# Decays kept as one row per head, the first tiles reordered, and an early pool for y and w_o in the last head unit of a lightning-attention kernel

## The chip, the cores and the metric

The kernel runs on one core of one Trainium2 chip. The core has a matmul engine (PE, with its weight loads shown apart as PEld), a vector engine (DVE), a scalar engine (ACT), GpSimd (POOL) and SP, which here only issues DMAs. The metric is the device time in microseconds of one execution; lower is better. All data are float32 in and out.

## The reference

The input is four sequences of 512 tokens with 512 features. It is normalised, goes through a linear attention with 16 heads of 128 and a decay per head, and the result is multiplied by a gate that comes from a router and added to the input.

```python
def reference(x, slope, w_qkv, w_gate, w_out, norm_w, router_w, router_b, expert_b):
    xn = layernorm(x)                                  # 4 x 512 x 512
    q, k, v = split(silu(xn @ w_qkv.T))                # 16 heads of 128
    # per head, in causal order, with s the head's slope:
    #   o[m] = sum over n <= m of exp(-s*(m-n)) * (q[m].k[n]) * v[n]
    o = norm_w * rms_normalise(o)                      # over all 2048 features
    a = (sigmoid(xn @ w_gate.T) * o) @ w_out.T
    p = softmax(xn @ router_w.T + router_b)            # 64 experts
    w, i = top_k(p, 8)
    g = silu(xn * sum(w) + sum_k w[k] * expert_b[i[k]])
    return x + a * g
```

The reference works in blocks of 64 tokens; the kernel uses blocks of 128 (`P`), which gives the same sums.

## The kernel before, in words

The program is one hand-written order of instructions for five engines. Each engine runs its own queue in program order; semaphores tie them together. The file's order is therefore the schedule: a list `after[0..6]` says what is emitted behind each of a unit's products.

**Products.** A float32 product is made of three passes over operands split into a high and a low part (`PASSES`; `split_hi` is a copy on ACT, `split_lo` a subtraction on DVE or POOL). A unit (`unit`, line 478) multiplies a 2x2 block of weights with a 2x2 block of tokens in seven products instead of eight (`PRODUCTS`: A11·B11, S2·T2, S1·T1, A12·B21, S3·T3, S4·B22, A22·T4), with six matmuls each. The S are sums of weight blocks, the T sums of token blocks. The first two units (`plain_unit`, line 519) take eight products instead, since their sums aren't there yet; in these T1 stands for the block B12. `do_deferred` emits the product with the sigmoid that an earlier sink has left open.

**V stage (lines 879 to 981).** Sixteen units, k = 0 to 15, make v. Eight token tiles (pairs of two sequences, 128 tokens each) go by in order with the first half of w_v (`ws[0]`), and then all again with the second half (`ws[1]`). Each tile is prepared while the one before is multiplied (`prepare`, line 816): `stats` and rstd (DVE, then POOL), `norms` (DVE), `turn` (transposes on PE, two copies on ACT, a store of the transposed tile), `sums`, `plain` and `more` (sums and splits of the token blocks), and `logits` (16 router matmuls). Four buffers hold x, four hold the finished v (`vout`).

**Decays.** `make_dist` builds a 128x256 table of token distances on POOL. `make_decays` takes its exponential for each head, 128x256, on ACT. `mask_decays` sets the upper triangle of the first half to zero on POOL and stores each head's table in DRAM by SP. In the head stage `load_decay` fetches one head's table.

**Head stage (lines 984 to 1062).** 48 units: for each of two pairs of sequences, a gate unit for two heads and then a q-k unit for each. `attention` of a head is emitted within the next unit: `scores_qk` behind product 1, `states` behind product 3, `attend` behind product 6. `attend` makes y = o * norm * gate (DVE), stores y in DRAM (SP), squares o (ACT) and adds the square up (POOL). Of the seven split token blocks of the second pair, four lie in the pool `xc` and three in `xa`. The PSUM pool `ps_sc` has three banks.

**Output stage (lines 1064 to 1123).** 32 steps, (sequence, head): y is loaded, split and multiplied with w_o (`o_head`, 12 matmuls a step). `ahead(i, loads, splits)` keeps loads and splits some steps ahead. The last head's attention sits in the first three steps (`last_steps`). In step 3 the head stage's pools are closed and the pool `late` is opened, which takes the loads from then on. `load_eb` and `split_eb` fetch and split the router's bias, `ffn` uses it.

Of the kernel before, what the change touches and what calls it, by code (L numbers as in the profile page):

```python
# [8 lines left out]
F32 = mybir.dt.float32  # L9
# [5 lines left out]
P = 128  # L15
# [35 lines left out]
def kernel(  # L51
# [61 lines left out]
    dist = const.tile([P, 2, P], F32, tag="dist", name="dist")  # L113
    rest_of = const.tile([P, 1], F32, tag="rest_of", name="rest_of")
# [5 lines left out]
    decay_d = [dram.tile([P, 2, P], F32, tag=f"decay{h}", name=f"decay_{h}") for h in range(NH)]  # L120
# [28 lines left out]

    def make_dist():  # L150
        nc.gpsimd.iota(
            dist[:, 0, :], pattern=[[-1, P]], base=0, channel_multiplier=1,
            allow_small_or_imprecise_dtypes=True,
        )
        nc.gpsimd.iota(
            dist[:, 1, :], pattern=[[-1, P]], base=-1, channel_multiplier=0,
            allow_small_or_imprecise_dtypes=True,
        )
        nc.gpsimd.iota(
            rest_of, pattern=[[0, 1]], base=1 - P, channel_multiplier=1,  # L160
            allow_small_or_imprecise_dtypes=True,
        )
        nc.gpsimd.tensor_scalar(dist[:, 0, :], dist[:, 0, :], 0.0, None, ALU.min)


    def make_decays(d, hs):
        for h in hs:
            nc.scalar.activation(d[h // 4][:, h % 4], dist, AF.Exp, scale=slopes[:, h : h + 1])

    def mask_decays(d, hs):  # L170
        for h in hs:
            nc.gpsimd.affine_select(
                d[h // 4][:, h % 4, 0], d[h // 4][:, h % 4, 0], pattern=[[1, P]],
                compare_op=ALU.is_ge, fill=0.0, base=0, channel_multiplier=-1,
            )
        for h in hs:
            nc.sync.dma_start(out=decay_d[h], in_=d[h // 4][:, h % 4])
# [69 lines left out]
    def transpose(stage, p, j, t):  # L247
# [6 lines left out]
        nc.scalar.copy(xfs[p, t][:, j], pt)  # L254
# [53 lines left out]
    def logits(stage, p, t):  # L308
        if t == 0:
            scores[p] = stage.tile([P, PB, NT, E], F32, tag="scores", name=f"scores_{p}", bufs=2)  # L310
        ps = ps_sc.tile([P, PB, E], F32, tag="sc", name=f"lg_{p}_{t}")
        for j in range(PB):
            for c in range(FC):
                nc.tensor.matmul(  # L314
                    ps[:, j], xfs[p, t][:, j, c, :], rw[:, c, :], start=(c == 0), stop=(c == FC - 1)
                )
        nc.vector.tensor_tensor(
# [331 lines left out]
    def load_decay(p, h, attp):  # L649
        dec[p, h] = attp.tile([P, 2, P], F32, tag="dec", name=f"dec_{p}_{h}", bufs=3)  # L650
        nc.sync.dma_start(out=dec[p, h], in_=decay_d[h])
# [86 lines left out]
    def load_eb(outp):  # L738
        ebs.append(outp.tile([P, F], F32, tag="x", name="raw_eb"))
# [29 lines left out]

    wos = {}  # L770
# [17 lines left out]
    def split_wo(h, wop, w):  # L788
        wr = wop.tile([P, 2, F], F32R, tag=f"wr{h}", name=f"wr_{h}", bufs=1)
# [96 lines left out]
    nc.scalar.activation(kdecay[:, 0:NT], mhalf, AF.Exp)  # L886
    nc.scalar.dma_start(out=slopes, in_=slope.to_broadcast([P, NH]))
# [3 lines left out]
    make_dist()  # L891
    warm_up(WARM)
# [3 lines left out]
    for n in ["A21"] + [n for n, _, _, _ in PRODUCTS]:  # L896
        ws[0].place(n)
    nc.scalar.activation(kdecay, slopes, AF.Exp, scale=rest_of[:, 0:1])
    nc.scalar.activation(bdecay, slopes, AF.Exp, scale=-float(P))
    ds = [  # L900
        sump.tile([P, KC * VW], F32, tag=f"sum{i}", name=f"mkdecay_{i}").rearrange(
            "p (h a m) -> p h a m", a=2, m=P
        ) for i in range(4)
    ]
    hs = range(0, 7), range(7, 12), range(12, NH)
    make_decays(ds, hs[0])
    prep[0]["stats"]()
    prep[0]["norms"]()
    ws[0].split_one("A11", nc.vector, hi=True)
    prep[0]["turn"]()  # L910
    load_pair(stage, *tiles[2])
    mask_decays(ds, hs[0])
    warm_up(6)
    prep[0]["sums"]()
    ws[0].split_one("A12", nc.gpsimd, 0)
    ws[0].split_one("A12", nc.vector, 1)
    prep[0]["logits"]()
    prep[1]["stats"]()
    ws[0].split_one("A21", nc.vector)
    make_decays(ds, hs[1])  # L920
    prep[1]["norms"]()
    load_pair(stage, *tiles[3])
    mask_decays(ds, hs[1])
# [245 lines left out]
```

## Time and profile before

| what | value |
|---|---|
| median of 3 runs | 1070.56 us (1069.88 to 1070.57) |
| the profiled execution's own time | 1069.32 us |
| its span, first to last instruction | 1067.6 us |
| instructions | 16505 |
| mean granted TensorE clock | 0.999 |
| DMA | 143.09 MB, 134 GB/s over the span |

The span is what the profiler saw between the first and the last instruction; the execution's own time is 1.7 us longer. The profile page gives busy time by engine, the DMA queues, and the costliest groups of instructions. Other views of the same trace show the busy time of each engine in chosen stretches, who waited for whom, the chain of work that ended last, and the instructions in order of time. A timeline line has the start, the duration, the engine, the line of the kernel, the operation, the tile written and the tiles read, and, in brackets, the idle time of the engine before it and what ended that. Times in these views are microseconds from the span's start. Consecutive instructions of one kind are merged ("x6"). The lines named most are L103 (`split_lo`), L100 (`split_hi`), L496 (matmul of a unit), L552 (product of `silu_of`) and L805 (`o_head`).

### The profile page before, as it was taken

The page shows a single profiled execution, that of the slowest core. Times are in us where ns is not written, and L with a number is a line of the kernel's source. Part 1 is how long each engine was busy: PE and PEld are TensorE (multiplying, and loading weights), DVE is VectorE, ACT ScalarE, POOL GpSimd, SP SyncE. Part 2 cuts the span into 40 slices and gives each one's busy share as a digit, 9 for nine tenths or more (in the row PEclk, how much of TensorE's full clock was granted, in tenths as well). Part 3 has the DMA queues.
Part 4 walks back from the last instruction along what each step waited for, and adds up shares of the span by engine and source line. Part 5 has one row for each costly group of instructions (what it writes and reads, how often), then busy time and mean ns, then how long its engine had stood idle before and what let it go on. Part 6 is the DMA issues. An engine that isn't in the chain of part 4 may idle for free.

```text
span 1067.6 us, 16505 instructions
## 1 busy us (share of the span) xinstructions
PE 1055.7 (99%) x5771; PEld 910.0 (85%) x5771; DVE 691.3 (65%) x1061; ACT 482.3 (45%) x938; POOL 731.0 (68%) x725
## 2 busy tenths in 40 slices
PE   9999999999999999999999999999999999999998
PEld 8788788888888888888888888888888887888886
DVE  5898776667576676655756656557566565754464
ACT  7545545544444444444444444444444444332221
POOL 6898793867788678777786787777867746612130
PEclk9999999999999999999999999999999999999999
DMA  8556745422422223234722242232222428364351
GB/s 273 194 181 241 268 153 178 140 92 85 139 84 94 83 94 111 95 124 171 278 85 66 84 128 85 85 125 88 85 75 88 135 80 285 94 189 173 88 197 50
DMA packets 105203, 143.09 MB, mean 134 GB/s; under 512 B 9120, under 2 KB 53536, under 8 KB 104224
## 3 DMA queue, kind: packets, MB, share of 16 engines
q1 hardware_dynamic: 104112, 141.33, 40.1%
q8 instruction: 46, 0.75, 0.3%
q10 hardware_dynamic: 1008, 0.70, 0.2%
q14 instruction: 37, 0.30, 0.1%
HBM read 91.14 MB, written 50.86 MB: 133 GB/s over the span
## 4 chain that ended last, share of the span: by engine, by line
PE 92%; DVE 3%; DMA 2%; ACT 1%; issue 1%; SPq 1%; POOL 0%; DVEq 0%; ACTq 0%; POOLq 0%
PE u_qk L496 28%; PE po L805 15%; PE u_g L496 14%; PE u_v L496 11%; PE o L702 5%; PE sa L665 5%; PE o L704 4%; PE ss L688 4%; PE kt L668 2%; DMA raw_v<-in_w_v_dram 1%; PE lg L314 1%; DVE vo_v L552 1%; PE pu L759 1%; DMA raw_eb<-in_expert_b_dram 1%; DVE sum_v L432 1%
## 5 line engine op out<-in xcount | busy, mean ns | idle before, releaser
L805 PE MATMUL po<-wr,yr 128*128 128x512 f32 (+1 forms) x777 | 179.7, 388 | 2.2 <-DVE u L798 1.0
L805 PEld LDWEIGHTS po<-wr,yr 128*128 128x128 f32 x777 | 144.2, 188 | 33.0 <-DVE u L798 1.2
L496 PE MATMUL u_qk<-blk_T,ws_qk 128*128 128x512 f32 x576 | 147.1, 395 | 0.0
L714 POOL TENSOR_TENSOR sqs<-sqs,sq 128x512 f32<-128x512 f32 x60 | 78.8, 1314 | 77.2 <-ACT sq L713 77.2
L496 PEld LDWEIGHTS u_qk<-blk_T,ws_qk 128*128 128x128 f32 x576 | 105.7, 188 | 20.4
L103 POOL TENSOR_TENSOR ws_qk<-sum_qk,ws_qk 128x512 fp32r<-128x512 f32 x64 | 82.9, 1297 | 30.4 <-ACT ws_qk L100 29.4
L103 DVE TENSOR_TENSOR yr<-yin,yr 128x512 fp32r<-128x512 f32 x64 | 69.1, 1095 | 47.0 <-ACT yr L100 47.0
L496 PE MATMUL u_qk<-blk_B,wa_qk 128*128 128x512 f32 x384 | 99.2, 393 | 0.0
L552 DVE TENSOR_TENSOR k<-k,sg_k 128x512 f32<-128x512 f32 x64 | 90.8, 1418 | 2.4 <-ACT sg_k L549 2.2
L702 PE MATMUL o<-at,vin 128*128 128x128 f32 x512 | 88.4, 275 | 0.0
L496 PEld LDWEIGHTS u_qk<-blk_B,wa_qk 128*128 128x128 f32 x384 | 70.9, 188 | 14.2
L692 DVE SCALAR_TENSOR_TENSOR st<-st,bdecay,ss 128x128 f32<-128x128 f32 x128 | 41.7, 346 | 60.7 <-ACT st L690 58.4
L549 ACT ACTIVATE sg_k<-k 128x512 f32<-128x512 f32 x64 | 40.5, 632 | 86.4 <-DVE k L487 86.4
L702 PEld LDWEIGHTS o<-at,vin 128*128 128x128 f32 x512 | 74.9, 191 | 2.5
L496 PE MATMUL u_g<-blk_T,ws_g 128*128 128x512 f32 x288 | 76.0, 400 | 0.0
L103 POOL TENSOR_TENSOR ws_g<-sum_g,ws_g 128x512 fp32r<-128x512 f32 x32 | 42.7, 1334 | 46.4 <-ACT ws_g L100 46.4
L704 PE MATMUL o<-qd,st 128*128 128x128 f32 x384 | 74.2, 275 | 0.0
L713 ACT ACTIVATE sq<-o 128x512 f32<-128x512 f32 x60 | 35.9, 598 | 72.3 <-POOL sqs L714 43.5
L767 POOL TENSOR_TENSOR u<-u,sgu 128x512 f32<-128x512 f32 x16 | 20.7, 1292 | 69.7 <-ACT sgu L766 60.4
L706 DVE SCALAR_TENSOR_TENSOR y<-o,nw,gt 128x512 f32<-128x512 f32 x64 | 47.6, 747 | 31.7 <-PE o L704 30.1
L665 PE MATMUL sa<-q,k 128*128 128x128 f32 x512 | 67.7, 275 | 0.2 <-DVE k L552 0.2
L665 PEld LDWEIGHTS sa<-q,k 128*128 128x128 f32 x512 | 64.3, 191 | 3.5 <-DVE q L552 0.7
(182 smaller groups left out, 2429.0 us busy)
## 6 DMA issues: line engine op xcount, KB each, us to landing
v<-vo_v SPq DMA_DIRECT2D x64, 256.0 KB, 2.0
raw_qk<-in_w_head_dram SPq DMA_DIRECT2D x64, 256.0 KB, 4.0
vin<-v SPq DMA_DIRECT2D x64, 256.0 KB, 3.6
y<-y SPq DMA_DIRECT2D x64, 256.0 KB, 2.1
yin<-y SPq DMA_DIRECT2D x64, 256.0 KB, 3.1
x<-in_x_dram SPq DMA_DIRECT2D x32, 256.0 KB, 4.6
raw_g<-in_w_head_dram SPq DMA_DIRECT2D x32, 256.0 KB, 3.1
raw_v<-in_w_v_dram SPq DMA_DIRECT2D x16, 256.0 KB, 5.3
```

The lines of the kernel that those rows point to most:

```text
L103: eng.tensor_tensor(lo, src, hi.bitcast(F32), ALU.subtract)
L496: nc.tensor.matmul(ps, lhsT, rhs, start=(first and c == 0 and n == 0), stop=(c == KC - 1 and n == len(PASSES) - 1), skip_group_check=not f ...
L549: nc.scalar.activation(sg, src, AF.Sigmoid)
L552: nc.vector.tensor_tensor(dst, src, sg, ALU.mult)
L665: nc.tensor.matmul(pa[:, c], k[:, c], q[:, c], start=True, stop=True)
L688: nc.tensor.matmul(ps[:, c], kd[s][:, c], v_of(b, h, c), start=True, stop=True)
L692: nc.vector.scalar_tensor_tensor(r[:, c], r[:, c - 1], bdecay[:, h : h + 1], ps[:, c], ALU.mult, ALU.add)
L702: nc.tensor.matmul(o, v_of(b, h, c), at[s][:, c], start=True, stop=(c == 0))
L704: nc.tensor.matmul(o, st[s][:, c - 1], qd[s][:, c - 1], start=False, stop=True)
L706: nc.vector.scalar_tensor_tensor(y, po, nw[:, h : h + 1], gts[s], ALU.mult, ALU.mult)
L714: nc.gpsimd.tensor_tensor(sq[b], sq[b], s1, ALU.add)
L805: nc.tensor.matmul(pos[t][:, c], yr[:, yi, bass.ts(t, P)], wos[h][:, wi, c], start=(h == 0 and n == 0), stop=(h in stops and n == len(PASS ...
```

## The change

**Decays as one row per head.** The table of a head depends only on the difference of two token positions. The change keeps one row of 256 values per head, 16x256, with zeros in its first 127 places: one exponential for all heads, one memset for the mask. `slope_of`, a column of 16 slopes, is loaded for it. `keep_rows` stores the rows in DRAM in unit 2; `keep_decay` copies a head's row 128 times, DRAM to DRAM, six heads a unit in units 13 to 15. `load_decay` reads two pieces: the first with a step of 255 elements from row to row, so that each row is shifted by one against the row above, the second straight.

**First tiles reordered.** A sigmoid on a small tile follows the exponentials. For tile 0 the transposes of both sequences come first; DVE copies the first out of PSUM, ACT splits B11 straight from PSUM, and POOL makes its low part. The router matmuls of the second sequence move into unit 0. The order of A12's halves on DVE and POOL is exchanged. Tile 1's normalisation comes before the split of A21. Tile 2's statistics are emitted ahead of tile 1's `turn`, and the normalisation of tiles 2 and 3 ahead of the other work of its slot. The splits of S4 of the second half come one product later.

**A pool for y and w_o in the last head unit.** `xc` gets a stack of its own, which is closed behind product 3 of the last head unit; a pool `op2` of four buffers is opened there. Loads and splits of the steps 2 and later use it instead of `late`. Six steps are loaded and three split by the end of the unit. The router's bias is loaded in the unit (into a w_o buffer) and split in step 3. w_o of the heads 4 to 6 goes into the blocks of `xa`, of the later ones into `late`.

```diff
-    dist = const.tile([P, 2, P], F32, tag="dist", name="dist")
+    W = 2 * P
+    decay_row = const.tile([NH, W], F32, tag="decay_row", name="decay_row")
+    by_row = const.tile([P, 2], F32, tag="rest_of", name="rest_of")
+    rest_of, slope_of = by_row[:, 0:1], by_row[0:NH, 1:2]
...
+    def make_decays():
+        nc.scalar.activation(decay_row, decay_row, AF.Exp, scale=slope_of)
+        nc.scalar.activation(kdecay, slopes, AF.Exp, scale=rest_of)
+        nc.scalar.activation(bdecay, slopes, AF.Exp, scale=-float(P))
+        nc.gpsimd.memset(decay_row[:, 0 : P - 1], 0.0)
+
+    def keep_rows():
+        nc.sync.dma_start(out=rows_d, in_=decay_row)
+
+    def keep_decay(h):
+        nc.sync.dma_start(out=decay_d[h], in_=rows_d[h : h + 1].to_broadcast([P, W]))
...
     def load_decay(p, h, attp):
         dec[p, h] = attp.tile([P, 2, P], F32, tag="dec", name=f"dec_{p}_{h}", bufs=3)
-        nc.sync.dma_start(out=dec[p, h], in_=decay_d[h])
+        rows = decay_d[h].rearrange("n m -> (n m)")[P - 1 : P - 1 + P * (W - 1)]
+        nc.sync.dma_start(
+            out=dec[p, h][:, 0], in_=rows.rearrange("(n m) -> n m", m=W - 1)[:, 0:P]
+        )
+        nc.sync.dma_start(out=dec[p, h][:, 1], in_=decay_d[h][:, P:W])
...
-        ebs.append(outp.tile([P, F], F32, tag="x", name="raw_eb"))
+        ebs.append(outp.tile([P, F], F32, tag="woin", name="raw_eb"))
...
+    def split_wo(h, w):
+        pool_, tag = (op, f"wr{h}") if h < 4 else (xa, f"x{h - 4}") if h < 4 + NX else (late, f"wr{h}")
+        wr = pool_.tile([P, 2, F], F32R, tag=tag, name=f"wr_{h}", bufs=1)
...
+    nc.scalar.dma_start(out=slope_of, in_=slope.rearrange("o h -> h o"))
     nc.scalar.dma_start(out=slopes, in_=slope.to_broadcast([P, NH]))
...
+    make_decays()
+
+    nc.scalar.activation(sig, mhalf, AF.Sigmoid)
     prep[0]["stats"]()
     prep[0]["norms"]()
+
+    pt = [transpose(stage, 0, j, 0, False) for j in range(PB)]
+    nc.vector.tensor_copy(xfs[0, 0][:, 0], pt[0])
+    b11, b12, b21, b22 = halves(xfs[0, 0])
+    split_hi(blocks[0, "B11"][:, 0, 0], pt[0][:, 0:KC])
     ws[0].split_one("A11", nc.vector, hi=True)
-    prep[0]["turn"]()
+    split_lo(nc.gpsimd, blocks[0, "B11"][:, 0, 1], b11, blocks[0, "B11"][:, 0, 0])
+    nc.scalar.copy(xfs[0, 0][:, 1], pt[1])
+    nc.sync.dma_start(out=xf_d[0], in_=xfs[0, 0])
     load_pair(stage, *tiles[2])
-    mask_decays(ds, hs[0])
     warm_up(6)
-    prep[0]["sums"]()
-    ws[0].split_one("A12", nc.gpsimd, 0)
-    ws[0].split_one("A12", nc.vector, 1)
-    prep[0]["logits"]()
+    split_blocks(0, 0, nc.vector, (("T1", b12), ("B21", b21), ("B22", b22)))
+    ws[0].split_one("A12", nc.vector, 0)
+    ws[0].split_one("A12", nc.gpsimd, 1)
+    logits(stage, 0, 0, [0])
     prep[1]["stats"]()
+    prep[1]["norms"]()
     ws[0].split_one("A21", nc.vector)
-    make_decays(ds, hs[1])
-    prep[1]["norms"]()
     load_pair(stage, *tiles[3])
-    mask_decays(ds, hs[1])
     ws[0].split_one("A22", nc.gpsimd)
...
+            if k == 0:
+                after[1].insert(0, prep[2]["stats"])
             after[1].append(prep[k + 1]["sums"])
             if k + 2 < n1:
-                after[1].append(prep[k + 2]["stats"])
-                after[4].append(prep[k + 2]["norms"])
+                if k:
+                    after[1].append(prep[k + 2]["stats"])
+                after[4 if k > 1 else 3].append(prep[k + 2]["norms"])
...
+        if k == 0:
+            after[0].append(lambda: logits(stage, 0, 0, [1]))
...
-            ("S4", n1, 0, nc.vector, 0), ("S4", n1, 1, nc.vector, 1), ("A22", n1, 0, nc.gpsimd, None),
+            ("S4", n1, 1, nc.vector, 0), ("S4", n1, 2, nc.vector, 1), ("A22", n1, 0, nc.gpsimd, None),
...
+        if k == NP_FIRST:
+            after[0].append(keep_rows)
+        if n1 + NT < k < n1 + 2 * NT:
+            for j in range(1, len(PRODUCTS)):
+                h = (k - n1 - NT - 1) * (len(PRODUCTS) - 1) + j - 1
+                if h < NH:
+                    after[j].append(lambda h=h: keep_decay(h))
...
         while nload < min(i + loads, len(steps)):
             b, h = steps[nload]
+            from_ = op if nload < 2 else op2
...
         if i == len(todo) - 1:
             ahead(0, 2, 0)
-            after[3].append(lambda: ahead(0, 2, 1))
-            after[5].append(lambda: ahead(0, 3, 2))
+
+
+            def more():
+                nonlocal op2
+                xc_stack.close()
+                op2 = left(o_stack, "o2", 4)
+                ahead(0, 4, 1)
+            after[3].append(more)
+            after[4].append(lambda: ahead(0, 4, 2))
+            after[5].append(lambda: load_eb(op))
+            after[6].append(lambda: ahead(0, 6, 3))
...
         if h < NH - 1:
-            ahead(i, *((3, 2) if late is None else (6, 3)))
+            ahead(i, 6, 3)
...
             if i == 3:
-                load_eb(late)
-            if i == 5:
                 split_eb(late)
```

## The prediction

> **What bounds the kernel now.** I read the page first, then busy time by stage, then PE's waits, then the timeline where PE waits.
>
> ```profile
> PE 1055.7 (99%) x5771; PEld 910.0 (85%) x5771; DVE 691.3 (65%) x1061; ACT 482.3 (45%) x938; POOL 731.0 (68%) x725
> ...
> 190.00:800.00 610.00, 610.00 (x3581) 536.29 (x3580) 390.92 (x638) 287.73 (x561) 466.33 (x455) 1.00 0.34 109
> ```
>
> Columns of the second line: stretch, length, busy PE, PEld, DVE, ACT, POOL, granted clock, DMA share, GB/s. PE has no gap for 610 us and the clock is full, and the change leaves PE's real work alone. So a gain can come only from the stretches where PE waits:
>
> ```profile
> 25.00:41.00 16.00, 15.25 (x84) 12.73 (x84) 13.59 (x21) 8.77 (x18) 12.59 (x13) 1.00 0.60 214
> 41.00:46.00 5.00, 4.58 (x24) 3.22 (x23) 4.72 (x7) 1.91 (x4) 5.00 (x6) 1.00 0.02 6
> 80.00:125.00 45.00, 43.74 (x216) 36.23 (x214) 38.42 (x54) 24.52 (x45) 36.94 (x35) 1.00 0.74 256
> 162.00:191.00 29.00, 29.00 (x129) 24.03 (x128) 18.84 (x29) 15.10 (x25) 9.94 (x11) 1.00 0.48 168
> 884.00:899.00 15.00, 12.72 (x52) 9.20 (x51) 6.22 (x7) 8.10 (x14) 10.21 (x8) 1.00 0.91 300
> ```
>
> Busy PE is flattered by modelled ends, so I count losses against the dense rate: 42 matmuls in 9.52 us (190.72 in the chain), 227 ns each; a transpose 111 ns; the 16 router matmuls 1.73 us.
>
> Place 1, the start. PE waits for a late normalisation of tile 2:
>
> ```profile
> 27.85 1.16 POOL L238 TENSOR_TENSOR rstd<-lnv,mhalf 128x2 f32<-128x2 f32 x1
> 29.04 1.00 DVE L204 TENSOR_SCALAR x<-x,stats,rstd 128x512 f32<-128x512 f32 x2
> 29.73 1.08 PE L253 MATMUL pt<-ident,x 128*128 128x128 f32 x8 [0.75 <-DVE x L204]
> ```
>
> Unit 1 runs from 25.91 to 40.67, 14.76 us, for 48 matmuls, 8 transposes and 16 router matmuls (10.90 + 0.89 + 1.73 = 13.52): 1.24 lost, 0.98 of it at this wait (the six matmuls from 27.39 end at 28.75, the transposes start at 29.73). From 40.67 to 49.56 PE does 30 matmuls and 8 transposes (7.70): 1.19 lost, to tile 3's normalisation and to a product freeing a bank at 45.18.
>
> Place 2, the first unit of the second V half: S3·T3 needs a bank that a_v frees, and a_v is queued on DVE behind a piece of S4:
>
> ```profile
> 117.99 0.68 DVE L103 TENSOR_TENSOR w_S_v<-sum_v,w_S_v 128x512 fp32r<-128x512 f32 x1
> 118.59 0.68 DVE L487 TENSOR_TENSOR a_v<-u_v,s_v 128x512 f32<-128x512 f32 x1
> 119.32 1.66 PE L496 MATMUL u_v<-w_S_v,blk_T 128*128 128x512 f32 x6 [1.15 <-DVE a_v L487]
> ```
>
> Place 3, the entry into the output stage: steps 4 to 6 wait for their splits, and the router bias arrives last.
>
> ```profile
> 888.57 8.01 PE L805 MATMUL po<-wr,yr 128*128 128x512 f32 x34 [0.63 <-POOL wr L103]
> ...
> 889.34 6.61 DMA raw_eb<-in_expert_b_dram
> ```
>
> From 883.57 to 898.58 are 15.01 us for 48 output matmuls and 2 of the router's (11.35): 3.66 lost.
>
> **Part 1, the start.** Removed: 16 exponentials on ACT (16 x 0.49 = 7.9 us), 16 masks on POOL (2.93 + 1.72 + 1.02 = 5.7), 16 stores of 128 KB on SP (12.83 to 25.0). Added: one exponential of 16x256 (0.49), a memset (0.10 by the others), one more tiny load on ACT's queue, and a sigmoid that brings the table load at 20.36 forward. ACT and POOL weren't what PE waited for between 12.0 and 25.9, so the removal itself buys little; it buys what the reordering allows. On SP, the loads of x tiles 2 and 3 no longer have the decay stores between them.
>
> The head, step by step. Slope column: nearest row is the slope load, 4.1 us from 0.93, so 5.0 (the queue's worst row, 6.4, gives 7.3). ACT: exp to 5.5, kdecay and bdecay (0.31, 0.20) to 6.1, table load 1.28, sigmoid 0.21: 7.6. POOL's memset, behind exp, holds rstd of tile 0 at most from 5.71 to 5.8, while DVE is busy with statistics until 6.97: free. [...] Here the load at 20.36 is followed by a sigmoid at 21.65[...]. By the row ACT is free at 7.6[...]; either is before ACT's next work at 9.15.
>
> That 9.15: norm of the second half ends at 8.44, DVE then copies pt[0] out (no such row; the nearest, L487 from PSUM, 0.69; between 0.54 and 0.75). ACT's B11 split reads the same PSUM tile. At L713 ACT's square starts only when DVE's read of the same tile is done ("1.06 <-DVE y L706"), so I let it wait. B11 hi 9.6, its lo on POOL (0.73) 10.4; A11 hi 10.15 and 10.7, lo on DVE 10.9 and 11.5; xf 11.25; T1 hi 11.6, lo 12.05; B21, B22 to 12.85; A12 hi 13.45, its first lo 14.2. PE: 6 warm-ups to 9.8, 8 router matmuls to 10.7 (10.24 and 12.04 before), A11·B11 and A11·T1 to 13.4, the other 8 to 14.3, A12's 12 to 17.0. Each operand is there in time. But then tile 1: statistics follow A12's split on DVE, 14.2 to 16.3 (2.1 as at 13.68), rstd 17.0, normalise from 17.1: the transposes start at 17.65, against 17.80. Unit 1 starts at 25.8 against 25.91: **0.1**.
>
> The gain comes next. Tile 2's statistics are put ahead of tile 1's transpose work: DVE 20.4 to 22.5, rstd 23.2, normalised by 25.7; PE asks at 28.5. The 0.98 goes. New queueing: tile 1's low parts on POOL stand behind this rstd (23.2); B11's is wanted at 26.0, ready at 23.9. For 40.67 to 49.56 DVE arrives some 2 us ahead and norms stand before S3: I take half of 1.19, since DVE is 94% busy there: 0.6. **Start: 1.7** (0 to 2.6).
>
> **Part 2, S4 a step later.** a_v moves up by 0.6, S4's pieces are done by 120.7, wanted from 120.1 + 0.45 and 121.2. **0.5** (0 to 1.15).
>
> **Part 3, decays from one row.** SP gets a 16 KB store, 16 copies from DRAM to DRAM in the last three V units, and two loads a head instead of one: 32 extra issues of 0.5 us, in a stage where SP waits 397 us for y alone; the raw weights behind them on SP are loaded two units ahead. The decay of a head is loaded at 195.0 and read at 213.7; landing 4.2 leaves 14 us of cover. Its first half is rows 1020 bytes apart[...]; uncovered, it would be up to 4.2 us a head. The copies: no DRAM-to-DRAM row. q1's 104112 packets took 40.1% of 16 engines, 66 ns each, so 128 packets are 0.53 us of all engines; twice that if read and write add. 16 copies: 8 to 17 us, against 52% of 29 us free, 15. The V stores have four buffers, a unit's worth. **0.** Raw weights for unit g0 land perhaps 3 us later than at 177.26; ACT reads them at 183.07.
>
> **Part 4, the last head unit.** The xc blocks are last read by A12·B21, over at 859.7. Then y and w_o of steps 2, 3 load at once (862.87 and 870.11 before), the second split moves from after product 5 to after 4, the bias loads during the unit, the third split comes behind the attention. On SP these loads stand ahead of head 14's two y stores: four issues of 0.42 to 861.5, two of the bias (0.70, 0.59) once POOL has freed w_o's first buffer at 864.0, to 865.3; y is stored from 869.0, so nothing waits. w_o of heads 4 to 6 goes to xa's blocks, last read at 865.1, long before. Steps 3 to 6 then find operands: POOL (wr 1.3 to 1.7 each, qd and squares between) has step 5's part at 888.8, wanted near 890; steps 6, 7 at 891.4, 892.7, wanted 892.7, 895.5. The bias is split at step 3. The 3.66 goes.
>
> But the third split adds a wait. Its ACT half queues behind head 14's squares, its DVE half stands ahead of the last k product, which scores of head 15 need:
>
> ```profile
> 868.28 1.40 DVE L706 SCALAR_TENSOR_TENSOR y<-o,nw,gt 128x512 f32<-128x512 f32 x2
> 869.60 0.68 DVE L552 TENSOR_TENSOR k<-k,sg_k 128x512 f32<-128x512 f32 x1
> 871.45 0.60 ACT L713 ACTIVATE sq<-o 128x512 f32<-128x512 f32 x1 [1.80 <-POOL sqs L714]
> 872.18 1.08 PE L665 MATMUL sa<-q,k 128*128 128x128 f32 x8
> ```
>
> With y starting a little earlier: square 868.8 to 869.4, POOL's add 1.3 to 870.8, second square 871.4, yr hi 871.9, yr lo 872.65, k 873.3. PE wants it at 872.35: a new wait of 0.95 (0.6 to 1.7 with POOL's add at 1.69). at, behind k, still frees the bank before the second kt. **End: 3.66 - 0.95 = 2.7** (0 to 3.7).
>
> **Sum.** 1.7 + 0.5 + 2.7 = 4.9. The profiled execution took 1069.32 (span 1067.6 and 1.7 around it); it would be 1064.4, span 1062.7. The median of the runs is 1.24 above it, so 1065.7.
>
> **Rivals.**
> (a) The start gives nothing: the slope column lands late, or tile 1's chain just moves on. For it: DVE and POOL are near full at 41 to 46. Against: 5.7 us come off POOL. 0.5 + 2.7 are left: 1070.56 - 3.2 = 1067.4.
> (b) The end gives nothing: POOL or ACT, in order, is late again at steps 4 to 6, or the new wait grows. For it: my margins are 1 to 2 us on POOL. 1.7 + 0.5 are left: 1070.56 - 2.2 = 1068.4.
> (c) Slower, by the 16 copies. Beyond 15 us of free engine time plus one unit of buffered stores (9.5), the queue holds up V stores, then DVE, then PE. It decides at 24.5/16 = 1.5 us a copy; at 2.3 us the excess is 16 x 2.3 - 24.5 = 12.3 and the time 1065.7 + 12.3 = 1078.0. Against: 0.53 us by the packets; for: nothing in the trace copies DRAM to DRAM.
> (d) The change doesn't do what it says: both ends move their waits only, 0.5 is left: 1070.0.
>
> **How the numbers follow.** 0.2%, 2.1 us, is about what a measurement of this kernel can tell from no change: faster means under 1068.4. Forecast 0.57 (1063.4 to 1067.5), all faster; (a) 0.15, 0.14 faster; (b) 0.12, half faster, half same; (c) 0.09, slower; (d) 0.07, same. Faster 0.77, same 0.14, slower 0.09. The range, 1063.4 to 1069.0, holds the forecast, (a) and most of (b).
>
> **What would show it.** Right: no wait of pt for x near 28; S3·T3's wait at the second half down to about 0.5; output matmuls dense from step 3 to the first router matmul; one new wait of about 1 us, sa for k, behind yr. Wrong: gaps in the V units at 162 to 191, B11 waiting beyond 12, or po still waiting for wr.

## The result, and the profile after

The changed kernel takes 1068.93 us, the median of 22 runs (1066.02 to 1071.60), beside 1070.01 for the kernel before on the same chip: a ratio of 0.9987, 95% interval 0.9982 to 0.9993. By the ratio it is faster by 1.4 us (0.7 to 1.9; the medians are 1.1 apart), where 4.9 was forecast. Its profiled execution took 1068.67 us (span 1066.9), 0.65 less than that of before.

The busy shares of the whole run hardly move (PE 99% in both), so they tell nothing. In the changed kernel the lines L487, L496, L552, L665 and L805 are L493, L502, L558, L675 and L818. Of the tiles below, sa are the scores q·k, at the scores times the decays, kt the transposed k, qd q times the decays, yr and wr the split y and w_o, po the output's sums.

Busy time by stage, the same five stretches as before (stretch, length, busy PE, PEld, DVE, ACT, POOL, granted clock, DMA share, GB/s):

```profile
25.00:41.00 16.00, 16.00 (x88) 13.66 (x87) 13.30 (x21) 7.50 (x15) 13.07 (x14) 1.00 0.39 133
41.00:46.00 5.00, 4.00 (x18) 2.94 (x17) 4.53 (x10) 3.28 (x7) 5.00 (x5) 1.00 0.28 105
80.00:125.00 45.00, 44.87 (x216) 37.03 (x215) 38.43 (x56) 24.66 (x47) 36.92 (x34) 1.00 0.76 269
162.00:191.00 29.00, 28.95 (x128) 23.64 (x127) 18.59 (x28) 14.50 (x24) 9.56 (x10) 1.00 0.77 234
884.00:899.00 15.00, 15.00 (x76) 12.56 (x75) 10.96 (x8) 7.04 (x13) 12.36 (x8) 1.00 0.72 240
```

PE's gaps at 25 to 41 and 884 to 899 are gone, most of the one at 80 to 125 too. One at 41 to 46 has grown, and the DMA share at 162 to 191 went from 0.48 to 0.77. PE's waits over the whole run show what came instead:

```profile
PE sa L675 <- DVE k L558: 3.2, 2, 3.0
PE warm L150 <- POOL ident masks.py:199: 1.4, 1, 1.4
PE u_v L502 <- DVE vo_v L558: 1.0, 1, 1.0
PE po L818 <- DVE u L811: 1.0, 1, 1.0
```

The wait for k was to be about 1 us; it is 3. The timeline there, the last head's scores behind output step 0 (start, duration, engine, operation; in brackets the idle time before it and who ended it):

```profile
869.27 1.27 POOL L724 TENSOR_TENSOR sqs<-sqs,sq 128x512 f32<-128x512 f32 x1 [0.71 <-ACT sq L723]
...
869.73 1.36 DVE L103 TENSOR_TENSOR yr<-yin,yr 128x512 fp32r<-128x512 f32 x1 [2.52 <-ACT yr L100]
...
870.49 1.72 POOL L103 TENSOR_TENSOR wr<-woin,wr 128x512 fp32r<-128x512 f32 x1
871.01 1.75 DVE L558 TENSOR_TENSOR k<-k,sg_k 128x512 f32<-128x512 f32 x1
...
872.91 2.04 PE L675 MATMUL sa<-q,k 128*128 128x128 f32 x8 [2.96 <-DVE k L558]
```

The low part of the third split (yr) and the k product stand on DVE one behind the other, and take 1.36 and 1.75 us. The forecast had about 0.7 for each. The eight scores then take 2.04 us; before, eight took 1.08. Busy time by microsecond says why (the number behind POOL's is the granted clock):

```profile
872.00:873.00 1.00, 0.09 (x1) 0.12 (x1) 1.00 (x2) 0.00 (x0) 1.00 (x2) 0.93 0.81 221
873.00:874.00 1.00, 1.00 (x5) 1.00 (x6) 0.36 (x1) 0.00 (x0) 1.00 (x2) 0.50 0.78 242
874.00:875.00 1.00, 1.00 (x7) 1.00 (x7) 0.01 (x1) 0.00 (x0) 0.57 (x1) 0.50 0.37 139
875.00:876.00 1.00, 1.00 (x5) 0.90 (x4) 0.68 (x1) 0.37 (x1) 0.00 (x0) 0.50 0.00 0
```

After the 3 us without work the granted clock is 0.50 for three of these rows. PE looks fully busy in these rows; it does the same work at about half the speed (2.04 us for the eight scores against 1.08).

**Where the time went, place by place.** What one kernel is ahead of the other when the same instruction starts:

| place | before | after | ahead | gained since the row above |
|---|---|---|---|---|
| unit 1, A11·B11 | 25.91 | 24.81 | 1.10 | 1.10 |
| unit 2, first product | 40.67 | 38.55 | 2.12 | 1.02 |
| unit 2, router matmuls begin | 49.40 | 47.57 | 1.83 | -0.29 |
| second V half, S4·B22 | 121.09 | 117.87 | 3.22 | 1.39 |
| first gate unit | 190.55 | 187.95 | 2.60 | -0.62 |
| output step 0 | 868.15 | 865.74 | 2.41 | -0.19 |
| output matmuls behind the first bias matmuls | 898.42 | 897.26 | 1.16 | -1.25 |

The start and S4 bring 2.4, which the forecast had at 2.2. The end loses 1.25, where 2.7 was to be gained. So the question is where the 3.66 of steps 4 to 6 went. They are recovered, all but 0.1, and spent again a few microseconds earlier; the 48 output matmuls of steps 3 to 6 are one piece:

```profile
885.70 11.27 PE L818 MATMUL po<-wr,yr 128*128 128x512 f32 x48
```

### The profile page after: what moved, and what is told of

Its sections match the earlier page's. It is cut to its first block, busy times and chain, and to the rows that moved or that the text cites. A ratio compares the mean times of both kernels' runs of the same rounds, so it can differ in the third digit from the quotient of the medians.

```text
span 1066.9 us, 16491 instructions
## 1 busy us (share of the span) xinstructions
PE 1056.2 (99%) x5771; PEld 910.9 (85%) x5771; DVE 695.6 (65%) x1061; ACT 476.1 (45%) x923; POOL 727.3 (68%) x710
## 4 chain that ended last, share of the span: by engine, by line
PE 93%; DVE 3%; DMA 2%; POOL 1%; SPq 1%; issue 1%; ACT 1%; DVEq 0%; ACTq 0%
PE u_qk L502 28%; PE po L818 16%; PE u_g L502 14%; PE u_v L502 11%; PE sa L675 5%; PE o L712 5%; PE ss L698 4%; PE o L714 4%; PE kt L678 2%; DMA raw_v<-in_w_v_dram 1%; PE lg L318 1%; PE pu L769 1%; DMA v<-vo_v 1%; DVE k L558 1%; POOL ts L268 0%
## 5 line engine op out<-in xcount | busy, mean ns | idle before, releaser
L818 PE MATMUL po<-wr,yr 128*128 128x512 f32 (+1 forms) x777 | 179.5, 389 | 1.0 <-DVE u L811 1.0
L818 PEld LDWEIGHTS po<-wr,yr 128*128 128x128 f32 x777 | 144.5, 188 | 31.2 <-DVE u L811 1.2
L502 PE MATMUL u_qk<-blk_T,ws_qk 128*128 128x512 f32 x576 | 147.1, 395 | 0.0
L502 PEld LDWEIGHTS u_qk<-blk_T,ws_qk 128*128 128x128 f32 x576 | 105.7, 188 | 20.5
L103 DVE TENSOR_TENSOR yr<-yin,yr 128x512 fp32r<-128x512 f32 x64 | 71.5, 1127 | 50.1 <-ACT yr L100 50.0
L502 PE MATMUL u_qk<-blk_B,wa_qk 128*128 128x512 f32 x384 | 99.1, 393 | 0.0
L558 DVE TENSOR_TENSOR k<-k,sg_k 128x512 f32<-128x512 f32 x64 | 92.3, 1442 | 2.4 <-ACT sg_k L555 2.2
L502 PEld LDWEIGHTS u_qk<-blk_B,wa_qk 128*128 128x128 f32 x384 | 70.9, 188 | 14.2
L502 PE MATMUL u_g<-blk_T,ws_g 128*128 128x512 f32 x288 | 76.0, 399 | 0.0
L675 PE MATMUL sa<-q,k 128*128 128x128 f32 x512 | 68.7, 278 | 3.2 <-DVE k L558 3.2
L675 PEld LDWEIGHTS sa<-q,k 128*128 128x128 f32 x512 | 65.1, 193 | 6.6 <-issue 3.2
```

The costliest lines, as they stand in the source:

```text
L103: eng.tensor_tensor(lo, src, hi.bitcast(F32), ALU.subtract)
L502: nc.tensor.matmul(ps, lhsT, rhs, start=(first and c == 0 and n == 0), stop=(c == KC - 1 and n == len(PASSES) - 1), skip_group_check=not f ...
L558: nc.vector.tensor_tensor(dst, src, sg, ALU.mult)
L675: nc.tensor.matmul(pa[:, c], k[:, c], q[:, c], start=True, stop=True)
L818: nc.tensor.matmul(pos[t][:, c], yr[:, yi, bass.ts(t, P)], wos[h][:, wi, c], start=(h == 0 and n == 0), stop=(h in stops and n == len(PASS ...
```

## The experiments

Theory: at the end, the third split in front of the k product makes a wait of 3 us, lengthened by POOL, and the wait makes the clock fall. Rivals: the clock falls for another reason; the early third split is needed by the later steps, so the wait can't be had back; what was gained at the start is chance. All ratios are to the kernel before on the same chip.

**k_first: the k product ahead of the split.**

```diff
-            after[6].append(lambda: ahead(0, 6, 3))
+            after[6].append(lambda: (do_deferred(), ahead(0, 6, 3)))
```

> The changed kernel with the last k product emitted ahead of the third split (order on DVE and ACT alone is changed). Theory (the third split in front of k makes the wait, and the wait makes the clock fall): sa of the last head follows kt without a wait, under 0.7 us of it left; granted clock 1.00 from 860 to 880; output matmuls of step 1 back at 2.7 us per 12; 3.0 + 1.9 = 4.9 us less than the changed kernel, about 1064.0, 6 us under the kernel before. Rival 1 (the low clock has nothing to do with the wait): 0.50 stays somewhere near 873, only 3.0 us less, about 1066. Rival 2 (the split behind k comes too late for step 2): a new wait of po for yr or wr of 1 to 2 us, about 1065 to 1066.

1065.39 us, ratio 0.9959 (0.9947 to 0.9971). The k product takes 0.68 at 868.36, the wait for it falls to 0.2, and the clock is 1.00 throughout. But the split now stands ahead of another operation:

```profile
871.36 1.36 DVE L103 TENSOR_TENSOR yr<-yin,yr 128x512 fp32r<-128x512 f32 x1 [2.32 <-ACT yr L100]
872.64 1.28 DVE L680 TENSOR_TENSOR at<-sa,dec 128x512 f32<-128x512 f32 x2
```

```profile
873.38 0.55 PE L678 MATMUL kt<-ident,k 128*128 128x128 f32 x3 [1.32 <-DVE at L680]
```

The transposes of k wait 1.32 us for a PSUM bank that at frees, and at is queued behind yr. That is neither rival as written: the split is in the way wherever it stands there. (This profile also shows one late start, 1.2 us of waits at 18.8 and 20.5, that none of the others has.)

**split_later: the third split in step 1, behind the scores.**

```diff
-            after[6].append(lambda: ahead(0, 6, 3))
+            after[6].append(lambda: ahead(0, 6, 2))
...
-            ahead(i, 6, 3)
+            ahead(i, 6, 3 if i else 2)
```

> The changed kernel with the third split moved behind the last head's scores (into output step 1, where the kernel before has it); the early loads stay. Theory: no wait of sa for k, clock 1.00, steps 2 to 6 still dense since the loads and the other splits are early: about 1064.0, equal to k_first within 0.5 us. Rival (the early third split is what removed the waits of steps 4 to 6): po waits return, up to 3.7 us, about 1067 to 1068.

1063.34 us, ratio 0.9944 (0.9931 to 0.9957): some 4.6 us under the changed kernel, by the two ratios. The wait is down to 0.2:

```profile
868.05 1.05 PE L675 MATMUL sa<-q,k 128*128 128x128 f32 x8
...
869.27 1.06 PE L675 MATMUL sa<-q,k 128*128 128x128 f32 x8
...
880.35 11.27 PE L818 MATMUL po<-wr,yr 128*128 128x512 f32 x48
```

Steps 3 to 6 stay dense (11.27 us for 48). So the early loads and the earlier other splits remove the waits of steps 4 to 6; the third split's early place adds nothing there but the wait.

**start_only and end_only: each half of the change alone.** The first is the changed kernel with the hunks of the output stage and the last head unit taken back, the second the kernel before with only these.

> The changed kernel with the output stage and the last head unit as they were before: the start, S4 and the decays alone are changed. Theory (the start and S4 give 2.4, the end costs 1.2): 2.4 us under the kernel before, about 1067.6, with the last head's first output matmul near 865.7 as in the changed kernel, the steps 4 to 6 waiting as before. Rival (0.9 us of the start is a lucky landing of the first x tile in one profile): 1.5 us under, about 1068.5, and a first x landing near 4.5 in its profile.

> The kernel before with the changed last head unit and output stage alone; start, S4 and decays as before. Theory (the end recovers 3.7 at steps 4 to 6 and loses 3.0 to the wait for k and up to 1.9 to the clock): from the last head's first output matmul on 1.2 us longer than the kernel before, sa waiting 2 to 3 us for k, steps 4 to 6 dense; about 1071.0. Rival (what the end costs in the changed kernel comes only with the earlier start): no loss, 1067 to 1069. Beside it, its start is the start of before once more: if the first statistics wait for x until 4.5 again, the order of that program makes it; if 3.5, the one profile of before was unlucky by 1 us there.

start_only: 1067.07 us, ratio 0.9979 (0.9969 to 0.9988), 2.2 us under before. end_only: 1070.41, ratio 0.9999 (0.9991 to 1.0007), no difference; its profile has the wait (2.96 behind k) and the clock at 0.50 again. So the end is worth nothing as it stands and 3.7 us in split_later's order, the difference between the ratios of split_later and start_only (by their intervals some 1.7 either way). The lengths of the two pieces of the output stage, by the timelines, tell the same (26.69 us in split_later, 30.27 in before):

| kernel | step 0 to step 3 | step 3 to the output matmuls behind the first bias |
|---|---|---|
| before | 15.16 | 15.11 |
| start_only | 15.17 | 15.70 |
| changed | 19.96 | 11.56 |
| changed, second profile | 18.34 | 11.57 |
| end_only | 19.95 | 11.56 |
| k_first | 16.64 | 11.61 |
| split_later | 15.12 | 11.57 |

**filler, filler_again and after_again: the clock.** 24 transposes that nobody reads are put between the two groups of scores, so that PE has work while it would wait. Both this kernel and the changed one were profiled twice.

```diff
-        [lambda: scores_qk(b1, hl, attp), lambda: scores_qk(b0, hl, attp)],
+        [lambda: scores_qk(b1, hl, attp), lambda: warm_up(24), lambda: scores_qk(b0, hl, attp)],
```

> The changed kernel with 24 transposes of the identity (2.66 us of PE work that nobody reads) put between the two score groups, in the wait. Theory (PE idle for 3 us is what lowers the granted clock): the wait of sa shrinks to about 0.3 to 0.5 us behind the filler, sa still starts near 872.9, the clock stays 1.00, and the next 8 scores, 3 transposes and 12 output matmuls take 0.91, 0.49 and 2.74 us again: 1.9 us less than the changed kernel, about 1067.0. Rival (the clock falls for another reason): 0.50 near 873 stays, the time is the changed kernel's, 1068.9.

> The kernel of run filler once more, for a second profile. Theory (the late landing of wTin that took back 1.7 us in its first profile is chance): clock 1.00 at 862 to 880, no wait of pu for wTin over 0.5. Rival (the filler's timing makes that load late): again 1 us or more of waits for wTin.

> The changed kernel once more, for a second profile. Theory: sa waits 2.9 to 3.0 us for k again, and the clock falls to 0.50 for about 3 us behind it, in most executions though not in all (it did not in run s4_back); first x statistics near 3.5. Rival (the fall was chance): clock 1.00.

filler: 1068.53 us, ratio 0.9990 (0.9984 to 0.9997); filler_again 1067.72 and after_again 1066.63 in single runs. In both profiles of the filler the scores start as late as without it, and at full clock; here filler's:

```profile
872.73 1.13 PE L675 MATMUL sa<-q,k 128*128 128x128 f32 x8 [0.38 <-DVE k L558]
...
873.00:874.00 1.00, 1.00 (x12) 1.00 (x10) 0.29 (x2) 0.00 (x0) 1.00 (x2) 1.00 0.63 152
```

The clock's mean over a run is 0.999 or 1.000 in all 21 timed runs of the filler, where the changed kernel's 22 runs have 0.996 to 0.999, 0.9976 in the mean. So at this place it is the idle time (2.96 us in the changed kernel, 0.38 in filler) that lets the clock fall. (A run's mean alone doesn't tell the place: slope_column, below, has no such wait and a full clock in its profile, and 7 of its 14 runs are at 0.996 or 0.997; where they lose it is open.) It doesn't fall every time: after_again waits as long with the clock at 1.00,

```profile
872.76 1.13 PE L675 MATMUL sa<-q,k 128*128 128x128 f32 x8 [2.98 <-DVE k L558]
```

and so did s4_back (2.95, below). In the changed kernel's first profile, end_only, stats_back and rw_first it fell, with waits of 2.96. Worked out from the clock of each microsecond, the low stretch is 3.4 us long in each of the four, and begins between 0.1 us before and 1.1 us after the wait's end. Its price is the difference in the table, 19.96 against 18.34: 1.6 us.

The time of the filler is not 1.9 less, though. Both its profiles show a wait that the changed kernel doesn't have:

```profile
935.63 0.73 PE L769 MATMUL pu<-ebs,wTin 128*128 128x512 f32 x2 [1.23 <-DMA wTin<-wTd]
```

That is the rival of filler_again. With a second, shorter wait of the kind it comes to 1.7 us in filler and 1.4 in filler_again, about the 1.6 that the full clock saves. Why a load of transposed router weights lands later there is open.

**wo_later: w_o's part of the third split, on ACT and POOL, behind the scores.** The y part (`False` leaves w_o out) stays ahead of k on DVE, all loads stay.

```diff
-            after[6].append(lambda: ahead(0, 6, 3))
+            after[6].append(lambda: ahead(0, 6, 3, False))
...
+            if i == 0:
+                split_wo(2, ow.pop(0))
```

> The changed kernel with POOL's and ACT's part of the third split (w_o of head 2) behind the last head's scores; the y part stays where the change put it, ahead of k on DVE, and the loads too. Theory (POOL working beside DVE makes the two DVE operations long): yr lo still 1.0 to 1.4 beside POOL's add of the squares, k back at 0.7 to 0.9, the wait of sa 1.8 to 2.1 instead of 2.96, the clock 1.00, 1.1 to 3 us less than the changed kernel: 1066 to 1067.8. Rival (DMA traffic, 0.8 to 1.0 of the engines there, makes them long): k stays at 1.75 and the wait at 2.96, time as the changed kernel's, 1068.9.

1068.98 us, ratio 0.9987 (0.9977 to 0.9997), no change; the wait is 2.68, k 1.47. The clock is 1.00 in the profile, but its execution is one of the shorter (1066.66), and the 14 runs have 0.9976 in the mean, as the changed kernel's. The theory's number failed: POOL, free of the split, did the next thing in its queue (qd, at 869.74) beside k. But another place of this run separates POOL from the DMA traffic. DVE's next two splits, and POOL beside them:

```profile
874.53 2.97 POOL L103 TENSOR_TENSOR wr<-woin,wr 128x512 fp32r<-128x512 f32 x2 [1.94 <-ACT wr L100]
...
875.00 1.36 DVE L103 TENSOR_TENSOR yr<-yin,yr 128x512 fp32r<-128x512 f32 x1 [1.28 <-ACT yr L100]
...
878.40 0.68 DVE L103 TENSOR_TENSOR yr<-yin,yr 128x512 fp32r<-128x512 f32 x1
...
878.84 1.39 POOL L103 TENSOR_TENSOR wr<-woin,wr 128x512 fp32r<-128x512 f32 x1 [1.34 <-ACT wr L100]
```

```profile
874.00:875.00 1.00, 1.00 (x6) 0.80 (x5) 0.00 (x0) 1.00 (x3) 0.47 (x1) 1.00 0.00 0
875.00:876.00 1.00, 1.00 (x6) 0.82 (x5) 0.99 (x1) 0.49 (x1) 1.00 (x2) 1.00 0.00 0
878.00:879.00 1.00, 1.00 (x6) 0.84 (x5) 0.96 (x3) 0.77 (x2) 0.16 (x1) 1.00 0.80 262
```

The same DVE operation takes 1.36 where POOL is already at work and 0.68 where POOL comes later, and no DMA runs at all beside the long one, while the short one has a DMA share of 0.80 beside it. DMA traffic is out as the cause. Moreover the end of the long ones follows POOL's: in the changed kernel POOL's add ends at 870.54 and yr at 871.09, POOL's wr at 872.21 and k at 872.76; in k_first the add ends at 872.17 and yr at 872.72. Each time DVE is done 0.55 us after the POOL operation that had begun before it. Each of these DVE operations, all with both inputs in SBUF, began behind one of POOL's and ended only behind its end. The sums from PSUM beside POOL (L493 at 860.35 in the changed kernel, 0.68) have one SBUF input and aren't lengthened: the changed kernel's 32 of that kind (k from u_qk and e_qk) take 0.66 to 0.69. Why they end so much later no view shows.

**s4_back: S4 at steps 0 and 1 again.**

```diff
-            ("S4", n1, 1, nc.vector, 0), ("S4", n1, 2, nc.vector, 1), ("A22", n1, 0, nc.gpsimd, None),
+            ("S4", n1, 0, nc.vector, 0), ("S4", n1, 1, nc.vector, 1), ("A22", n1, 0, nc.gpsimd, None),
```

> The changed kernel with the two pieces of S4 back at steps 0 and 1 of the first unit of the second V half. Prediction's step: S3.T3 waits 0.5 us longer for a_v, 1069.4. By the two traces (3.22 gained at the second half against 1.83 before it) rather 1.4: S3.T3 waits 1.1 or more for a_v and the time is 1070.3. Rival (the earlier start alone removes that wait): no wait, 1068.9.

1069.46 us, ratio 0.9996 (0.9987 to 1.0004). Beside the changed kernel's 0.9987 the intervals overlap, so the time can't tell 0.5 from 1.4. The wait can:

```profile
117.38 1.66 PE L502 MATMUL u_v<-w_S_v,blk_T 128*128 128x512 f32 x6 [1.45 <-DVE a_v L493]
```

Moving S4 removes 1.45, all of it (the changed kernel runs this product at 116.19 without a wait); the forecast left 0.65 of the wait standing.

**stats_back: tile 2's statistics and the two normalisations where they were.**

```diff
-            if k == 0:
-                after[1].insert(0, prep[2]["stats"])
...
-                after[4 if k > 1 else 3].append(prep[k + 2]["norms"])
+                after[4].append(prep[k + 2]["norms"])
```

> The changed kernel with tile 2's statistics behind tile 1's transpose work again and its normalisation at step 4. Theory (the order of tile 2's statistics is what removes the wait of the transposes in unit 1): pt near 28 waits 0.7 to 1 us for x, unit 2 starts 1.0 later, the time is up to 1.0 more, 1069.9. Rival (it is the lighter POOL and ACT that remove it): no wait, 1068.9.

1068.45 us, ratio 0.9980 (0.9971 to 0.9989), not slower than the changed kernel. The theory falls. No wait at 28 comes back:

```profile
27.77 1.03 PE L251 MATMUL pt<-ident,x 128*128 128x128 f32 x8
```

The transposes of the next two tiles stand at 40.02 and 52.41. In the changed kernel the three are at 27.67, 39.91 and 53.49, the last behind a wait of 1.00 (at 43.34) for a product of vo_v that is queued on DVE behind the early normalisation. Every profile with the new order has that wait (0.37 to 1.00 us), stats_back and best have not. So this reordering isn't what removes the wait at 28, and costs up to 1 us in unit 2. That the lighter ACT and POOL remove it, as the rival has it, fits, but isn't told apart from the other changes of the start.

**slope_twice, slope_column and rw_first: the first x tile.** It lands at 4.53 and 4.58 in the two profiles with the start of before, and at 3.4 to 3.8 in every profile of the changed start. The first two kernels are before with the slope column's load added ahead on ACT's queue, into a tile of its own or into the second column of rest_of; nothing reads it. rw_first is the changed kernel with the router weights first on that queue.

> The kernel before with one more load of 64 bytes (the slope column) ahead of the others on ACT's queue, as the changed kernel has it; nothing reads it. Theory (the router weights, issued 0.45 us later, no longer share the engines with the first x tile): the first statistics start near 3.5 instead of 4.5, unit 1 starts 0.3 to 0.9 earlier, the time is 0.3 to 0.9 less, 1069.5. Rival (something else in the changed start does it): 4.5, no change, 1070.2.

> The kernel of slope_twice with the slope column in the second column of the tile rest_of, so that no tile moves; still nothing reads it. Theory (slope_twice's 9.6 us came from moved addresses: its output products took 1.56 instead of 1.52 us per six in many places): all groups of six at 1.52 again, x of tile 0 lands near 3.6, unit 1 at 25.85, time as the kernel before, 1069.6, at most 0.3 less. Rival (the load itself costs it): 1079 again.

> The changed kernel with the router weights' load ahead of the two slope loads on ACT's queue. Theory (the early landing of the first x tile, which the changed order can use, is what moved unit 1 by 1.0 more than forecast): the first statistics wait for x until about 4.5, unit 1 starts near 25.7 instead of 24.8, tile 2 and 3 follow it, time 0.5 to 1.0 more than the changed kernel, about 1069.7. Rival (the order does it whatever x does): unit 1 at 24.8 to 25.1, 1068.9.

slope_twice: 1079.25 us, ratio 1.0089 (1.0075 to 1.0103). slope_column: 1070.13, ratio 1.0003 (0.9995 to 1.0011). rw_first: 1069.55, ratio 0.9989 (0.9980 to 0.9998), by the ratio the changed kernel's time; that it came near its theory's 1069.7 is no support. In slope_twice x lands at 3.60 and unit 1 starts at 25.85; in slope_column at 3.48 and 25.89. So with the additional load the landing is 1 us earlier, and in the old order unit 1 (25.91) gains next to nothing by it. In rw_first x lands at 3.79 with the router weights in front, so the theory of what the landing competes with falls; what moves it stays open. Unit 1 starts at 25.06 there, at 24.8 to 25.3 in all profiles of the changed start but k_first's.

The 9.6 us of slope_twice were not expected by anything here. Of the 8.8 us by which its profile is longer than that of before, 7.8 are in the head stage, in which PE waits for nothing new: most of the groups of six matmuls that took 1.52 us take 1.56.

```profile
596.21 1.52 PE L496 MATMUL u_qk<-blk_B,wa_qk 128*128 128x512 f32 x6
597.57 1.56 PE L496 MATMUL u_qk<-blk_T,ws_qk 128*128 128x512 f32 x6
```

slope_column issues the same loads and has 1.52 in these groups, as before has, and the time of before. What differs between the two is where the 4 bytes a partition lie: in a tile of their own, behind which other tiles can move, or in an existing one. No view shows the addresses, so that they are the cause is what is left over, not shown.

**both and best: a version that beats both.** both is split_later with the sixteen decay copies three V units earlier; best takes stats_back's order as well.

```diff
-        if n1 + NT < k < n1 + 2 * NT:
+        if n1 + 1 < k < n1 + 1 + NT:
...
-                h = (k - n1 - NT - 1) * (len(PRODUCTS) - 1) + j - 1
+                h = (k - n1 - 2) * (len(PRODUCTS) - 1) + j - 1
```

> The changed kernel with the third split in step 1 (as split_later) and the 16 decay copies three V units earlier, where the DMA share is 0.49, 0.49 and 0.29. Theory (the copies beside raw weights and V stores hold V stores up by 0 to 2 us near 180): copies land in under 4.4 us, V stores of the last units near 2 us again, no DVE wait for a V store, 0 to 0.6 us under split_later, about 1063.0. Rival (the copies collide with the reloaded tiles there): waits of PE for blocks or xf between 130 and 160, 1064 or more.

> The kernel of run both (third split in step 1, copies three units earlier) with tile 2's statistics and the normalisations of tiles 2 and 3 back where the kernel before has them, since the run stats_back had no wait of S1.T1 there. Theory (the reordering only moves the two normalisations ahead of a split and a product on DVE): S1.T1 in unit 2 starts without a wait, unit 3's transposes 0.4 us earlier than in both, the time 0.4 us less, about 1063.9. Rival (chance between profiles): a wait near 28 or 42 comes back, time as both, 1064.3.

both: 1064.32 us, ratio 0.9942 (0.9931 to 0.9954). best: 1062.89, ratio 0.9937 (0.9925 to 0.9949). They can't be told from split_later (0.9944) by time, so no gain over it is shown, but the waits that they were made for are gone. In the changed kernel DVE stood behind a V store that was late beside the copies and the raw weights of the gate units:

```profile
180.41 0.69 DVE L493 TENSOR_TENSOR vo_v<-u_v,a_v 128x512 f32<-128x512 f32 x1 [2.22 <-DMA v<-vo_v]
```

This wait of 1.8 to 2.5 us is in ten of the profiles with the copies there (start_only has none), and not in both and best. What it costs PE differs. From S4·B22 to the first gate unit PE takes 69.46 us in before and 69.49 in s4_back; 69.74 to 69.76 in start_only, both and best, which have S4 late and no such wait; 69.76 to 70.40 in the other kernels with S4 late, 70.08 in the changed one. So of the table's 0.62 some 0.3 come with the late S4, and 0.3 with the copies. PE's whole list of waits in best:

```profile
PE warm L150 <- POOL ident masks.py:199: 1.4, 1, 1.4
PE po L818 <- DVE u L811: 1.0, 1, 1.0
PE u_v L502 <- DVE a_v L493: 0.6, 1, 0.6
PE sa L675 <- DVE k L558: 0.2, 1, 0.2
```

The third line is new against both. stats_back has it too. With unit 2 no longer late, a_v is again what comes last at the second V half; so the gain in unit 2 is lost again there.

## Why the prediction was wrong

1068.93 lies inside the stated range, but at its far end (1069.0), which only rival (b) reaches, and above the 1068.4 under which the prediction would call it faster. The forecast itself missed by 3.5 of its 4.9 us.

**The end: the wait for k was mis-sized, and its consequence left out.** The step is "A new wait of 0.95 (0.6 to 1.7 with POOL's add at 1.69)". The mechanism and the place were right: sa waits for k, k behind yr, yr behind head 14's squares. By that working, and 2.41 us earlier, yr lo was to begin at 869.5; it began at 869.73. What failed is the length of the two DVE operations: 1.36 + 1.75 = 3.11 instead of 1.4 (871.9 to 873.3 in the working), which is 1.7 of the 2.0 by which the wait grew. The 0.68 was taken from one row, the k product at 869.60 of before, where POOL began 0.13 us later and its own operation was the long one (1.69, against 1.27 at 872.13):

```profile
869.73 1.69 POOL L714 TENSOR_TENSOR sqs<-sqs,sq 128x512 f32<-128x512 f32 x1 [1.92 <-ACT sq L713]
```

The prediction counted the 1.69 in its range, as POOL's own length, and not that the same can happen to DVE. The page of before had the warning, in its fifth part:

```profile
L103 DVE TENSOR_TENSOR yr<-yin,yr 128x512 fp32r<-128x512 f32 x64 | 69.1, 1095 | 47.0 <-ACT yr L100 47.0
...
L552 DVE TENSOR_TENSOR k<-k,sg_k 128x512 f32<-128x512 f32 x64 | 90.8, 1418 | 2.4 <-ACT sg_k L549 2.2
```

A k product takes 1418 ns in the mean of 64, and the medians (the middle one of the three numbers) are longer still:

```profile
L103 DVE TENSOR_TENSOR yr<-yin,yr x64: 673/1192/1780, 862.2 to 1050.1; 128x512 fp32r<-128x512 f32 x64
L552 DVE TENSOR_TENSOR k<-k,sg_k x64: 675/1710/1814, 209.0 to 869.6; 128x512 f32<-128x512 f32 x64
```

675 is the minimum. With these medians, 1.2 and 1.7, in place of 0.7 and 0.7, the wait comes out at 2.45.

The second omission: behind a wait of 3 us of PE (2.95 to 2.98) the granted clock halved (0.50) in four of the six profiles that have it, for 1.6 us more; behind 2.7 (wo_later) and 1.3 (k_first) it didn't, in the one profile that each has. The trace of before has no such wait in this stage and could not show it. With the wait taken at 0.95, the clock was put at nothing.

So the sum at the end was 3.55 recovered (15.11 to 11.56 in the table; 3.66 was nearly right), less 3.2 for the wait (15.16 to 18.34), less up to 1.6 of clock: between -1.25 and +0.4 where 2.7 was forecast. split_later's 3.6 in the table (3.7 by the ratios) is what the step brings without the wait. Rival (b), "the new wait grows", is what happened; it was priced at no more than the loss of the whole gain, and had 0.12.

**The start: the sum right by luck.** 2.2 was forecast with S4, and start_only measured 2.2 (1.3 to 3.3). But the parts were not right and cancel:
- "Unit 1 starts at 25.8 against 25.91: 0.1" was 0.6 to 1.1. The working started from the first statistics at 4.53, and everything behind it on DVE moved with the landing at 3.67: the second half was normalised at 7.71 and not at 8.44. That the landing counts in this order is argued from the chain; rw_first didn't bring the late landing back, so it isn't shown.
- "The 0.98 goes" is right, its reason wrong: it goes without the reordering (stats_back).
- "I take half of 1.19: 0.6" for 40.67 to 49.56 was -0.29: normalising early put a DVE operation ahead of the product that frees a bank. The 1.19 itself was 1.03, since 49.56 is the chain's date for what the timeline has at 49.40, and 40.67 is the timeline's.
- S4's 0.5 was 1.4 at that place, for the wait would have grown to 1.45 with the earlier start, over the bound of 1.15. Some 0.3 is lost again behind the late pieces of S4, which leaves 1.1.

**The decays: 0 was -0.3** in the changed profile and between 0 and -0.7 in the others. The copies land in a median of 4.4 us. Their engine time was near the estimate: the DMA share of 162 to 191 rose by 0.29, 8.4 us of all engines if all of it is theirs, the lower end of "8 to 17 us". But V stores issued behind raw weights and copies land late, one of them after 6.56 us (the median of the 64 is 2.1). That is rival (c) in small, far from its 1078. The two loads a head stay hidden, as forecast: PE's only listed wait in the head stage is one of 0.2 us for k, as before.

## What to carry to other kernels

Take an operation's duration from the group's mean or median, and a single row only when it is known what ran beside it: the DVE operations with two inputs in SBUF in the rows above took 0.68 us where no POOL operation was under way when they began, and 1.36 to 1.75 where one was. Before work is pulled ahead, list what stands behind it in each in-order queue and who waits for that; "earlier" was wrong here for the third split and for a normalisation, and right for the loads. A PE wait of some 3 us has to be priced with what the clock does after it (here 0.50 for 3.4 us in four profiles of six, 1.6 us). An edit that adds a tile is worth a run of its own.

## What the runs showed that was not expected

- In the rows above, DVE operations with two SBUF inputs end 0.55 us after the POOL operation that was under way when they began (1.36 to 1.75 so, 0.68 where none was). The other way round POOL's add takes 1.69 begun behind DVE's k product (before, 869.73), 1.27 at 872.13.
- Behind a PE gap of 3.0 us the clock was 0.50 for 3.4 us in four profiles and 1.00 in two, at a price of 1.6 us. The spread of the changed kernel's times, 1066.0 to 1071.6, isn't explained by that alone: its runs at a mean clock of 0.999 go from 1066.02 to 1070.07.
- One tile of 4 bytes a partition, unread, made the kernel 9.6 us slower (1079.25 against 1069.62); the same load into an added column of an existing tile cost nothing (1070.13 against 1069.97). That moved addresses are the cause is the author's guess, not shown: they were not read, and which operand's would matter was not tried.
- With one more 64-byte load ahead on ACT's queue the first x tile, on SP's queue, landed 1 us earlier (3.60 and 3.48 against 4.53 and 4.58, two profiles each); why is open.
